# Cross-attention on Trainium2: a pair's transposes in front of the next pair's scores, with the exponentials and the normalising passes behind the values' copies

## The chip, the cores and the metric

The kernel runs on one core of a Trainium2 chip. A core has five engines that work side by side: TensorE (matmuls; its weight loads are listed apart, as PEld), VectorE (DVE), ScalarE (ACT), GpSimd (POOL) and SyncE (SP), which here issues the transfers. Each engine runs its own list of instructions in order and waits on semaphores for the others. TensorE writes its results into PSUM, eight banks of 128 x 512 fp32; the other data lies in SBUF, and the rest in the chip's memory. The metric is the device time of one execution in microseconds; lower is better.

## The reference, cut to what matters

There are 16 sequences of 64 tokens with 512 features, so 1024 tokens, and a context of the same shape. The computation is

```python
def attention(xn, ctx, bias, mask):              # xn: layer-normed x
    q, k, v = xn @ Wq, ctx @ Wk, ctx @ Wv        # 32 heads of 128
    s = einsum('bqhd,bkhd->bhqk', q, k) / sqrt(128) + bias
    s = where(mask, s, -inf)
    p = where(mask, softmax(s), 0)
    return einsum('bhqk,bkhd->bqhd', p, v).reshape(...) @ Wo   # 4096 -> 512

x = x + attention(layernorm(x), ctx, fside, mask)
# base product, plus experts of rank 16 that a router of 15 outputs weighs (its 8 largest)
x = x + ffn(layernorm(x))
```

Everything is fp32. Each sequence attends only to its own 64 context tokens, so scores and values are many small products (64 x 64 for each sequence and head), while the four projections of 512 to 4096 features and back are large ones.

## The kernel before, in words

**Products.** A large product is done in a split form: `split` (L69 to L71) writes the high part of an operand with a ScalarE cast (named `gh`, `wh`, `oh`, after what is split) and the remainder with a VectorE subtraction (`gl`, `wl`, `ol`), and `mm3` (L256) issues three 128 x 512 matmuls, high by high, low by high, high by low. In the profile these are the L259 matmuls. The projections to keys, values and queries use a scheme with seven products in place of eight on 2 x 2 blocks. One of the seven, for the queries of a pair of heads, is called here a query step: six matmuls of L259.

**Stages.** Up to about 328 us the keys and values of all 32 heads are computed and stored in the chip's memory (`kd`, `vd`). Then comes the attention loop of L563 to L604, over 16 pairs of heads, and from about 737 us the feed-forward part.

**A pair.** The weights of a pair's query product are loaded by `load_pair` and added and split on GpSimd, ScalarE and VectorE; `Queries` (L512) runs the seven steps, one for each call, copying partial results from PSUM with ScalarE (`u`, L530, and `q21`) or VectorE (`q`, L537). `scores` (L456) issues 16 small matmuls for a head into one bank from the pool `pss`, scales them and adds the bias with the mask (`bm`) on VectorE (L465), takes the row maxima (`nm`, L467), calls eight exponentials on ScalarE (L470; each also reads out its row sums into `sme`), and then normalises on VectorE: reciprocal (L473), times `valid` (L474), and the product p times rc (L475). `transpose_p` (L478) transposes a head's probabilities with four 128 x 128 transposes of TensorE into a bank of `pss`, and copies them out on ScalarE (`pt`). `pv_mm` (L487) multiplies them by the values with 32 small matmuls for a head into two banks of the pool `psp`, and splits the results (`oh`, `ol`). `proj_o` (L503) multiplies one tile of 128 tokens of a pair's results by that pair's part of Wo, two sets of three matmuls, and VectorE adds the bank to `acc` (L510). There are eight such tiles, `t` = 0 to 7. The profile counts two instructions for each small matmul of scores and values, so a pair has 64 and 128 of them.

**Order.** An iteration of the loop begins with the values of the previous pair (L566), whose results its `proj_o` calls use. Then it follows a string of letters: S is the scores of both heads of this pair, with their softmax, and after it the loads of the next pair's keys (`load_k`) and bias (`bias_of`); Q is one step of the next pair's queries; O is `proj_o` for the next tile; T is the transposes of one head. The third Q also loads this pair's rows of Wo (`load_o`, `wh`, `wl`), the seventh the weights of the pair after the next. The string is "QSQQQQQTQT" in the first pair, "QSQQOOQOQOOQOQOTTO" in all between, "SOOOOOOTOT" in the last. A Tile scheduler puts each engine's instructions in order by priority, which is program order except under `tc.high_priority(offset=...)`, where an instruction counts as that much earlier (SOON is 200). `tc.issue_after(x)` puts what is in its block behind instruction x on the engines. In the trace of a steady pair TensorE does, in this order: the values, a query step, the scores, query steps and Wo products mixed, the transposes of both heads, and a last Wo product.

**Banks and buffers.** `psp` has six banks, which rotate among queries, values and Wo products (`bank()`), `pss` has two. SBUF blocks are drawn from pools by tag (L40): ten `raw`, eight `sn` (scores p, their transposed form pt, and u), nine `o`, eighteen `g`, five `v`, and two `bm`.

Of the kernel before, what the change touches and what calls it, by code (L numbers as in the profile page):

```python
# [9 lines left out]
F32 = mybir.dt.float32  # L10
# [5 lines left out]
ALU = mybir.AluOpType  # L16
# [3 lines left out]
P = 128  # L20
# [4 lines left out]
S = 64  # L25
# [10 lines left out]
SOON = 200  # L36
# [11 lines left out]
def xattn_ffn_kernel(ctx: ExitStack, tc: tile.TileContext, x, ctxT, wq, wk, wv, wo, fside, mask,  # L48
                     base_wT, base_b, arT, router_b, lora_b, expert_map, out):
    nc = tc.nc  # L50
# [12 lines left out]
    def bank(k=None):  # L63
        return psp.tile([P, 512], F32, tag="ps", name="ps")

    def blk(tag, name, dt=F32, shape=(P, 512)):
        return pools[tag].tile(list(shape), dt, tag=tag, name=name)

    def split(hi, lo, src, lo_eng=None):  # L69
        nc.scalar.copy(hi, src)  # L70
        (lo_eng or nc.vector).tensor_tensor(lo, src, hi.bitcast(F32), ALU.subtract)  # L71

    valid = small.tile([P, NT], F32, name="valid")
    nhalf = small.tile([P, NT], F32, name="nhalf")
# [34 lines left out]
    with ExitStack() as actx:  # L109
# [6 lines left out]
        def small_bank(name):  # L116
            return pss.tile([P, 512], F32, tag="s", name=name)
# [138 lines left out]
        def mm3(o, stat, mov, first, last):  # L256
            (sh, sl), (mh, ml) = stat, mov
            for n, (a, b) in enumerate(((sh, mh), (sl, mh), (sh, ml))):
                nc.tensor.matmul(o, lhsT=a, rhs=b, start=first and n == 0, stop=last and n == 2,  # L259
                                 skip_group_check=True)  # L260
# [86 lines left out]
        with tc.manual_schedule(engines={nc.tensor.engine}):  # L347
# [3 lines left out]
            with tc.manual_schedule(engines={nc.tensor.engine, nc.vector.engine, nc.scalar.engine}):  # L351
                gs[0][1] = [blk("g", f"g{c}", F32R, (P, 2, 256)) for c in "hl"]
                tc_[1] = [tp.tile([P, 2, HALF], F32R, tag=f"t1{c}", name=f"t1{c}") for c in "hl"]
                hi, lo = tc_[1]
# [60 lines left out]
            acc = None  # L415
# [17 lines left out]
            def load_v(p):  # L433
                v = []
                for w in range(4):
                    v.append(blk("v", "v", F32, (P, 2, 256)))
                    nc.sync.dma_start(out=v[w], in_=vd[p // 2][:, p % 2, 2 * w:2 * w + 2, :])
                return v

            def load_o(p):  # L440
                w = []
                for i in range(2):
                    s = blk("raw", "so")
                    nc.sync.dma_start(out=s, in_=wo[p, i])
                    hl = [blk("g", f"w{c}", F32R) for c in "hl"]
                    split(hl[0], hl[1], s)
                    w.append(hl)
                return w
# [7 lines left out]
            def scores(qT, kT, bm):  # L456
                ps = small_bank("pss").rearrange("p (t s) -> p t s", t=NT)
                for t in range(NT):
                    for a in range(2):
                        n = 4 * (t // 2) + 2 * a + t % 2  # L460
                        c = slice((n % 8) * S, (n % 8 + 1) * S)
                        nc.tensor.matmul(ps[a * S:(a + 1) * S, t, :], lhsT=qT[n // 8][:, c],  # L462
                                         rhs=kT[n // 8][:, c], start=True, stop=True)
                p = blk("sn", "p", F32, (P, NT, S))
                nc.vector.scalar_tensor_tensor(p, ps, scale, bm, ALU.mult, ALU.add)  # L465
                nm = sm.tile([P, NT], F32, tag="nm", name="nm")
                nc.vector.tensor_reduce(nm, p, AX.X, ALU.max, negate=True)  # L467
                sme = sm.tile([P, NT], F32, tag="sme", name="sme")
                for t in range(NT):
                    nc.scalar.activation(p[:, t, :], p[:, t, :], AF.Exp, bias=nm[:, t:t + 1],  # L470
                                         accum_out=sme[:, t:t + 1])
                rc = sm.tile([P, NT], F32, tag="rc", name="rc")
                nc.vector.reciprocal(rc, sme)  # L473
                nc.vector.tensor_tensor(rc, rc, valid, ALU.mult)  # L474
                nc.vector.tensor_tensor(p, p, rc.unsqueeze(2).to_broadcast([P, NT, S]), ALU.mult)  # L475
                return p

            def transpose_p(p):  # L478
                ps = small_bank("pst")
                for g in range(4):  # L480
                    nc.tensor.transpose(ps[:, g * P:(g + 1) * P],  # L481
                                        p[:, 2 * g:2 * g + 2, :].rearrange("p t k -> p (t k)"), ident)
                pt = blk("sn", "pt", F32, (P, NT, S))
                nc.scalar.copy(pt, ps.rearrange("p (u q) -> p u q", q=S))
                return pt

            def pv_mm(i, pt, v, home="o"):  # L487
                ps = [bank() for _ in range(2)]
                for u in range(NT):
                    for b in range(2):  # L490
                        r = slice(b * S, (b + 1) * S)
                        for d in range(0, P, S):
                            c = slice(i * P + d, i * P + d + S)
                            nc.tensor.matmul(ps[b][d:d + S, u * S:(u + 1) * S], lhsT=v[u // 2][r, u % 2, c],  # L494
                                             rhs=pt[r, u, :], start=True, stop=True)
                res = []
                for b in range(2):
                    hl = [blk(home, f"o{c}", F32R) for c in "hl"]
                    split(hl[0], hl[1], ps[b])
                    res.append(hl)  # L500
                return res

            def proj_o(t, cts, w):  # L503
                ps = bank()
                b, g = divmod(t, 4)
                c = slice(g * P, (g + 1) * P)
                for i, ct in enumerate(cts):
                    mm3(ps, [a[:, c] for a in ct[b]], w[i], i == 0, i == 1)
                with tc.high_priority(offset=SOON):
                    nc.vector.tensor_tensor(acc[:, t, :], acc[:, t, :], ps, ALU.add)  # L510

            class Queries:  # L512

# [33 lines left out]
            qs = Queries(load_pair(0), ORDER_Q)  # L547
            tx = Tokens(xT, nc.gpsimd).all(ORDER_Q)
            acc = ax.tile([P, NT, D], F32, tag="ax", name="acc")
            for t in range(0, NT, 2):  # L550
                nc.sync.dma_start(out=acc[:, t:t + 2, :], in_=x[t:t + 2].rearrange("t p d -> p t d"))
            for n, i in enumerate(winograd(mm_weights(tc_, ops[len(stages) - 1]), 2, emit_k(NQ - 1), order=ORDER_Q)):
                if n == 3:
                    ks = [load_k(0), load_k(1)]
                    with tc.issue_after(stored[-1].ins):
                        bms = [bias_of(0), bias_of(1)]
# [2 lines left out]
            nxt = Queries(load_pair(1), ORDER_1)  # L559
            qs(1)  # L560
            NP = H // 2
            pts = v = w = prev = None
            for p in range(NP):  # L563
                last = p + 1 == NP
                if pts is not None:
                    prev = ([pv_mm(i, pts[i], v) for i in range(2)], w)  # L566
                v = load_v(p)
                after = None
                steps = "SOOOOOOTOT" if last else "QSQQOOQOQOOQOQOTTO" if p else "QSQQQQQTQT"
                pts, t, n = [], 0, 0  # L570
                for c in steps:
                    if c == "S":
                        ps = [scores(qs.head(i), ks[i], bms[i]) for i in range(2)]
                        if not last:
                            ks = [load_k(2 * p + 2 + i) for i in range(2)]
                            bms = [bias_of(2 * p + 2 + i) for i in range(2)]
                    elif c == "Q":
                        nxt(1)
                        n += 1
                        if n == 3:  # L580
                            w = load_o(p)
                        if n == 7 and p + 2 < NP:
                            after = Queries(load_pair(p + 2), ORDER)
                        if n == 7 and p + 2 == NP:
                            sar = [blk("raw", "sar", F32, (P, 2, NB)) for _ in range(2)]
                            sbw = [blk("raw", "sbw") for _ in range(KC)]
                            slb = blk("g", "slb")
                            nc.sync.dma_start(out=slb, in_=lora_b)
                            for i in range(2):
                                nc.gpsimd.memset(sar[i][:, :, NAR:NB], 0.0)  # L590
                                nc.sync.dma_start(out=sar[i][:, :, 0:NAR], in_=arT[:, 2 * i:2 * i + 2])
                            for kc in range(KC):
                                nc.sync.dma_start(out=sbw[kc], in_=base_wT[:, kc])
                    elif c == "T":
                        pts.append(transpose_p(ps[len(pts)]))
                    else:
                        proj_o(t, *prev)
                        t += 1
                        if last and t == 2:
                            w = load_o(p)  # L600
                qs, nxt = nxt, after
            now = ([pv_mm(i, pts[i], v, "g") for i in range(2)], w)
            proj_o(t, *prev)
            prev = now  # L604

# [122 lines left out]
    def out_norm(t):  # L728
        proj_o(t, *prev)
        ffn_norm(t)  # L730
# [27 lines left out]
    with tc.manual_schedule(engines=fixed | {nc.vector.engine}):  # L758
        for t in range(NT):
# [6 lines left out]
            n = 1 if t else 2  # L766
            po = bank()[:, 0:NF - NA]
            ffn_mm(po, *x2s[t], B, range(n))
            hh, hl = ffn_turn(hw)
# [52 lines left out]
```

## Time and profile before

| what | before |
|---|---|
| median of three runs | 778.54 us (777.83 to 778.75) |
| the profiled execution's own time | 779.41 us |
| its span, from first to last instruction | 777.6 us |
| TensorE busy | 770.8 us, 99%, 6314 matmuls |
| TensorE weight loads | 642.1 us, 83% |
| VectorE busy | 574.3 us, 74%, 1036 instructions |
| ScalarE busy | 413.6 us, 53%, 1165 instructions |
| GpSimd busy | 134.9 us, 17%, 143 instructions |
| granted TensorE clock | 0.997 of full speed |
| moved by DMA | 120.48 MB, 155 GB/s on average |

How to read it: a row of the timeline or of the groups has the start (or nothing), the busy time or mean, the engine, the line, the operation, what is written and what is read by the program's names, the tile's size and the count; a bracket gives idle time before it and what ended that. Matmuls are pipelined and their ends are modelled, so two of them overlap in the rows, and the distance from one start to the next tells what one costs. The weight load of the next matmul runs beside the matmul before. A row of the busy time by stretch gives the length and then, for TensorE, weight loads, VectorE, ScalarE and GpSimd, the busy time with the number of instructions, and last the granted clock, the share of time in which the DMA engines were busy, and GB/s. A row of the chain gives start, length, engine, tile, line and count.

### The profile page before, as it was taken

Reading aid. Unit: us, or ns where it says so; the run is one execution under the profiler, and the core shown is the slowest. Engines: PE = TensorE matmul, PEld = TensorE weight load, DVE = VectorE, ACT = ScalarE, POOL = GpSimd, SP = SyncE. Lnnn points to the kernel's source line nnn. Section 1 sums busy time; section 2 is a strip of 40 time slices with the busy share of each in tenths; the row PEclk is TensorE's granted clock in tenths of the full one; section 3 lists DMA queues with packets and bytes.
Section 4 is the critical chain, followed back from the end, with each engine's and each line's share of the span. In section 5 each row is a group of like instructions: output and inputs, shape, how many; then the busy total and the mean of one; then the engine's idle time right before and its main releaser. Section 6 shows DMA issues by size and latency. Waiting matters only on the chain.

```text
span 777.6 us, 16694 instructions
## 1 busy us (share of the span) xinstructions
PE 770.8 (99%) x6314; PEld 642.1 (83%) x6314; DVE 574.3 (74%) x1036; ACT 413.6 (53%) x1165; POOL 134.9 (17%) x143
## 2 busy tenths in 40 slices
PE   8999999999999999999999999999999999999998
PEld 6888887888888888887888888888888888888898
DVE  6986666665665756787877787778777877779875
ACT  5664454545454545575564556455645564556461
POOL 0000000000000522133330332033203320310330
PEclk9999999999999999999999999999999999999999
DMA  6695646464536345474554355435543544352011
GB/s 243 227 294 179 195 161 209 131 208 151 203 120 204 122 140 200 166 243 140 185 164 122 110 178 165 129 104 176 164 138 96 176 164 131 103 176 70 1 53 58
DMA packets 74705, 120.48 MB, mean 155 GB/s; under 512 B 7680, under 2 KB 24832, under 8 KB 74624
## 3 DMA queue, kind: packets, MB, share of 16 engines
q1 hardware_dynamic: 74480, 119.36, 46.7%
q8 instruction: 49, 0.80, 0.4%
q14 instruction: 32, 0.26, 0.1%
q10 hardware_dynamic: 144, 0.06, 0.0%
HBM read 83.74 MB, written 35.65 MB: 154 GB/s over the span
## 4 chain that ended last, share of the span: by engine, by line
PE 95%; DVE 3%; ACT 1%; DMA 1%; issue 0%; POOL 0%; SPq 0%; DVEq 0%; ACTq 0%; POOLq 0%
PE ps L259 74%; PE yz L259 5%; PE ps L668 5%; PE pss L462 4%; PE ps L494 4%; PE pst L481 2%; DVE gl L71 1%; ACT p L470 1%; DMA cT<-in_ctxT 1%; PE pst L104 0%; DVE bs L634 0%; DVE wl L71 0%; PE pt L104 0%; DVE ol L71 0%; DVE acc L510 0%
## 5 line engine op out<-in xcount | busy, mean ns | idle before, releaser
L70 ACT CAST gh<-s 128x512 fp32r<-128x512 f32 (+1 forms) x128 | 65.6, 515 | 121.1 <-PE ps L259 112.3
L470 ACT ACTIVATE p<-p,nm 128x64 f32<-128x64 f32 x256 | 85.5, 336 | 31.3 <-DVE nm L467 31.3
L259 PE MATMUL ps<-wh,oh 128*128 128x512 f32 x256 | 101.3, 396 | 0.0
L510 DVE TENSOR_TENSOR acc<-acc,ps 128x512 f32<-128x512 f32 x128 | 85.9, 681 | 20.2 <-PE ps L259 20.0
L259 PE MATMUL ps<-wh,ol 128*128 128x512 f32 x256 | 99.8, 390 | 0.0
L259 PE MATMUL ps<-wl,oh 128*128 128x512 f32 x256 | 99.8, 390 | 0.0
L71 DVE TENSOR_TENSOR gl<-s,gh 128x512 fp32r<-128x512 f32 (+1 forms) x128 | 71.5, 562 | 32.9 <-ACT gh L70 31.8
L161 POOL TENSOR_TENSOR s<-rq 128x256 f32<-128x256 f32 x32 | 27.6, 863 | 262.8 <-DMA rq<-in_wq 127.9
L71 DVE TENSOR_TENSOR gl<-raw,gh 128x512 fp32r<-128x512 f32 x48 | 34.5, 722 | 36.5 <-ACT gh L70 26.1
L259 PEld LDWEIGHTS ps<-wl,oh 128*128 128x128 f32 x256 | 48.0, 188 | 10.0
L259 PEld LDWEIGHTS ps<-wh,ol 128*128 128x128 f32 x256 | 48.1, 188 | 9.7 <-DVE ol L71 0.4
L259 PEld LDWEIGHTS ps<-wh,oh 128*128 128x128 f32 x256 | 48.1, 188 | 9.5
L70 ACT CAST gh<-raw 128x512 fp32r<-128x512 f32 x48 | 29.7, 622 | 48.3 <-PE yz L259 29.3
L453 POOL TENSOR_TENSOR bm<-bm,maskb 128x512 f32<-128x512 f32 x32 | 48.2, 1526 | 28.9 <-DVE rc L474 21.5
L470 ACT ACTIVATION_READ_ACCUMULATOR p<-p,nm 128x1 f32 x256 | 48.2, 188 | 0.0
L71 DVE TENSOR_TENSOR ol<-ps,oh 128x512 fp32r<-128x512 f32 x64 | 39.9, 682 | 10.3 <-ACT oh L70 10.3
L96 POOL TENSOR_TENSOR rs<-rs,nhalf 128x1 f32<-128x1 f32 x8 | 4.4, 551 | 246.1 <-DVE rs L95 246.1
L537 DVE TENSOR_TENSOR q<-u,ps 128x512 f32<-128x512 f32 x48 | 32.6, 680 | 9.2 <-PE ps L259 8.9
L70 ACT CAST oh<-ps 128x512 fp32r<-128x512 f32 x64 | 33.2, 591 | 11.6 <-PE ps L494 11.6
L71 DVE TENSOR_TENSOR gl<-rq,gh 128x256 fp32r<-128x256 f32 x48 | 26.9, 562 | 15.4 <-ACT gh L70 15.4
L462 PEld LDWEIGHTS pss<-kT,q 128*64 128x64 f32 x1024 | 31.3, 138 | 5.7 <-PE ps L259 5.2
L475 DVE TENSOR_TENSOR p<-p,rc 128x512 f32<-128x512 f32 x32 | 34.9, 1092 | 1.1
(260 smaller groups left out, 2015.8 us busy)
## 6 DMA issues: line engine op xcount, KB each, us to landing
kd<-c SPq DMA_DIRECT2D x64, 256.0 KB, 2.2
vd<-c SPq DMA_DIRECT2D x64, 256.0 KB, 2.6
kT<-kd SPq DMA_DIRECT2D x64, 256.0 KB, 5.0
v<-vd SPq DMA_DIRECT2D x64, 256.0 KB, 4.3
raw<-in_wk SPq DMA_DIRECT2D x32, 256.0 KB, 4.0
raw<-in_wv SPq DMA_DIRECT2D x32, 256.0 KB, 4.1
rq<-in_wq SPq DMA_DIRECT2D x32, 256.0 KB, 4.7
bm<-in_fside SPq DMA_DIRECT2D x32, 256.0 KB, 5.0
```

Of the source, the lines that this page charges most:

```text
L70: nc.scalar.copy(hi, src)
L71: (lo_eng or nc.vector).tensor_tensor(lo, src, hi.bitcast(F32), ALU.subtract)
L161: self.eng.tensor_tensor(r, a, b, op)
L259: nc.tensor.matmul(o, lhsT=a, rhs=b, start=first and n == 0, stop=last and n == 2, skip_group_check=True)
L453: nc.gpsimd.tensor_tensor(bm, bm, maskb, ALU.add)
L462: nc.tensor.matmul(ps[a * S:(a + 1) * S, t, :], lhsT=qT[n // 8][:, c], rhs=kT[n // 8][:, c], start=True, stop=True)
L470: nc.scalar.activation(p[:, t, :], p[:, t, :], AF.Exp, bias=nm[:, t:t + 1], accum_out=sme[:, t:t + 1])
L475: nc.vector.tensor_tensor(p, p, rc.unsqueeze(2).to_broadcast([P, NT, S]), ALU.mult)
L494: nc.tensor.matmul(ps[b][d:d + S, u * S:(u + 1) * S], lhsT=v[u // 2][r, u % 2, c], rhs=pt[r, u, :], start=True, stop=True)
L510: nc.vector.tensor_tensor(acc[:, t, :], acc[:, t, :], ps, ALU.add)
L537: nc.vector.tensor_tensor(self.blocks[key], s[u], b[bk], ALU.add)
L668: nc.tensor.matmul(o, lhsT=a, rhs=b, start=start, stop=stop, skip_group_check=True)
```

## The change

The transposes leave the end of an iteration and go to the front of the next one, directly before its scores. `scores` is cut in three: scaling and maxima stay, the exponentials become `exps`, the normalising pass becomes `normed`. The values become a letter of the string, P: they are computed after the scores and one query step, and the exponentials of both heads are issued behind the last of the values' casts (`evicted` holds the last cast and the last subtraction). Each head's normalising pass is issued behind the addition of a certain O to `acc`: the third O for the first head, the fifth for the second, and in the last pair the third and fourth. The transposes draw a bank of `psp` instead of `pss`; their copy and the values' copies get a higher priority. The loads of Wo rows are placed behind the values' copies. A lower-case o is an O of the pair before, left over to be issued after P; the pair before the last has five Os and the last pair takes over the rest. The number of matmuls, exponentials, copies and bytes stays as it was.

```diff
     def split(hi, lo, src, lo_eng=None):
-        nc.scalar.copy(hi, src)
-        (lo_eng or nc.vector).tensor_tensor(lo, src, hi.bitcast(F32), ALU.subtract)
+        first = nc.scalar.copy(hi, src)
+        return first, (lo_eng or nc.vector).tensor_tensor(lo, src, hi.bitcast(F32), ALU.subtract)
 
     valid = small.tile([P, NT], F32, name="valid")
     nhalf = small.tile([P, NT], F32, name="nhalf")
@@ -465,10 +465,16 @@
                 nc.vector.scalar_tensor_tensor(p, ps, scale, bm, ALU.mult, ALU.add)
                 nm = sm.tile([P, NT], F32, tag="nm", name="nm")
                 nc.vector.tensor_reduce(nm, p, AX.X, ALU.max, negate=True)
+                return p, nm
+
+            def exps(p, nm):
                 sme = sm.tile([P, NT], F32, tag="sme", name="sme")
                 for t in range(NT):
                     nc.scalar.activation(p[:, t, :], p[:, t, :], AF.Exp, bias=nm[:, t:t + 1],
                                          accum_out=sme[:, t:t + 1])
+                return p, sme
+
+            def normed(p, sme):
                 rc = sm.tile([P, NT], F32, tag="rc", name="rc")
                 nc.vector.reciprocal(rc, sme)
                 nc.vector.tensor_tensor(rc, rc, valid, ALU.mult)
@@ -476,13 +482,16 @@
                 return p
 
             def transpose_p(p):
-                ps = small_bank("pst")
+                ps = bank()
                 for g in range(4):
                     nc.tensor.transpose(ps[:, g * P:(g + 1) * P],
                                         p[:, 2 * g:2 * g + 2, :].rearrange("p t k -> p (t k)"), ident)
                 pt = blk("sn", "pt", F32, (P, NT, S))
-                nc.scalar.copy(pt, ps.rearrange("p (u q) -> p u q", q=S))
+                with tc.high_priority(offset=SOON):
+                    nc.scalar.copy(pt, ps.rearrange("p (u q) -> p u q", q=S))
                 return pt
+
+            evicted = []
 
             def pv_mm(i, pt, v, home="o"):
                 ps = [bank() for _ in range(2)]
@@ -496,7 +505,8 @@
                 res = []
                 for b in range(2):
                     hl = [blk(home, f"o{c}", F32R) for c in "hl"]
-                    split(hl[0], hl[1], ps[b])
+                    with tc.high_priority(offset=2 * SOON):
+                        evicted[:] = split(hl[0], hl[1], ps[b])
                     res.append(hl)
                 return res
 
@@ -507,7 +517,7 @@
                 for i, ct in enumerate(cts):
                     mm3(ps, [a[:, c] for a in ct[b]], w[i], i == 0, i == 1)
                 with tc.high_priority(offset=SOON):
-                    nc.vector.tensor_tensor(acc[:, t, :], acc[:, t, :], ps, ALU.add)
+                    return nc.vector.tensor_tensor(acc[:, t, :], acc[:, t, :], ps, ALU.add)
 
             class Queries:
 
@@ -559,25 +569,36 @@
             nxt = Queries(load_pair(1), ORDER_1)
             qs(1)
             NP = H // 2
-            pts = v = w = prev = None
+            ps, pts, t, w, prev = [], [], 0, None, None
+            v = load_v(0)
             for p in range(NP):
                 last = p + 1 == NP
-                if pts is not None:
-                    prev = ([pv_mm(i, pts[i], v) for i in range(2)], w)
-                v = load_v(p)
                 after = None
-                steps = "SOOOOOOTOT" if last else "QSQQOOQOQOOQOQOTTO" if p else "QSQQQQQTQT"
-                pts, t, n = [], 0, 0
+                steps = ("TTSOPooOOOOOOTOT" if last else "TTSQPQQQOOQOQOQO" if p + 2 == NP else
+                         "TTSQPQQQOOQOOQOOQOO" if p > 1 else "TSQPQQQOOQOOQOOQOO" if p else "QSQQQQQTQ")
+                n = 0
                 for c in steps:
-                    if c == "S":
-                        ps = [scores(qs.head(i), ks[i], bms[i]) for i in range(2)]
+                    if c == "P":
+                        old, told = prev, t
+                        prev, t = ([pv_mm(i, pts[i], v, "g" if last else "o") for i in range(2)], w), 0
+                        pts = []
+                        v = load_v(p)
+                        with tc.issue_after(evicted[0].ins):
+                            soft = [exps(*s) for s in ss]
+                    elif c == "S":
+                        ss = [scores(qs.head(i), ks[i], bms[i]) for i in range(2)]
+                        if not p:
+                            ps = [normed(*exps(*s)) for s in ss]
                         if not last:
                             ks = [load_k(2 * p + 2 + i) for i in range(2)]
                             bms = [bias_of(2 * p + 2 + i) for i in range(2)]
                     elif c == "Q":
                         nxt(1)
                         n += 1
-                        if n == 3:
+                        if n == 3 and p:
+                            with tc.issue_after(evicted[0].ins), tc.issue_after(evicted[1].ins):
+                                w = load_o(p)
+                        elif n == 3:
                             w = load_o(p)
                         if n == 7 and p + 2 < NP:
                             after = Queries(load_pair(p + 2), ORDER)
@@ -592,14 +613,21 @@
                             for kc in range(KC):
                                 nc.sync.dma_start(out=sbw[kc], in_=base_wT[:, kc])
                     elif c == "T":
-                        pts.append(transpose_p(ps[len(pts)]))
+                        pts.append(transpose_p(ps.pop(0)))
                     else:
-                        proj_o(t, *prev)
+                        if c == "o":
+                            proj_o(told, *old)
+                            told += 1
+                            continue
+                        added = proj_o(t, *prev)
                         t += 1
+                        if t in (3, 5 - last):
+                            with tc.issue_after(added.ins):
+                                ps.append(normed(*soft.pop(0)))
                         if last and t == 2:
                             w = load_o(p)
                 qs, nxt = nxt, after
-            now = ([pv_mm(i, pts[i], v, "g") for i in range(2)], w)
+            now = ([pv_mm(i, pts[i], v) for i in range(2)], w)
             proj_o(t, *prev)
             prev = now
```

## The prediction

> **What bounds the kernel now.** I read the busy table first, then the busy time by stretch, then the chain of work in order of time, then TensorE's and VectorE's own timelines.
>
> ```profile
> PE   770.8 (99%) x6314; PEld 642.1 (83%) x6314; DVE 574.3 (74%) x1036; ACT 413.6 (53%) x1165; POOL 134.9 (17%) x143
> ...
> PE 95%; DVE 3%; ACT 1%; DMA 1%; issue 0%; POOL 0%; SPq 0%; DVEq 0%; ACTq 0%; POOLq 0%
> ```
>
> ```profile
> 328.00:371.00 43.00, 42.32 (x538) 34.46 (x536) 33.66 (x59) 28.15 (x104) 13.78 (x12) 1.00 0.60 196
> 371.00:705.00 334.00, 334.00 (x3749) 277.92 (x3752) 264.43 (x440) 184.17 (x661) 76.96 (x78) 1.00 0.46 145
> ```
>
> The second fence has pairs 0 and 1, then pairs 2 to 14. In the second stretch TensorE is busy for all of 334.00 us; in the first it misses 0.68 us. A busy TensorE may still hide gaps, so I go by spacing of starts. The chain of one steady pair:
>
> ```profile
> 442.77 0.87 PE pst L481 x8
> 443.64 1.38 PE ps L259 x6
> 445.02 2.02 PE ps L494 x128
> 447.04 1.59 PE ps L259 x6
> 448.64 2.02 PE pss L462 x64
> 450.65 17.93 PE ps L259 x78
> 468.58 0.87 PE pst L481 x8
> ```
>
> The period is 25.81 us, TensorE alone, and it repeats to 0.01 us in almost every pair. The change keeps every matmul, so it can win only (1) waits and (2) gaps where one kind of matmul follows another. TensorE's timeline shows both:
>
> ```profile
> 361.24 0.39 PE L259 MATMUL ps<-wl,oh 128*128 128x512 f32 x1
> 362.31 0.50 PE L259 MATMUL ps<-t3h,gh 128*128 128x512 f32 x1 [0.68 <-DVE q L537]
> ...
> 520.05 1.03 PE L481 MATMUL pst<-ident,p 128*128 128x128 f32 x8
> 520.84 0.48 PE L259 MATMUL ps<-wh,oh 128*128 128x512 f32 x1
> 521.15 0.40 PE L259 MATMUL ps<-wh,ol 128*128 128x512 f32 x1
> 521.39 0.39 PE L259 MATMUL ps<-wl,oh 128*128 128x512 f32 x1
> ...
> 717.79 0.60 PE L481 MATMUL pst<-ident,p 128*128 128x128 f32 x4
> 718.31 0.40 PE L494 MATMUL ps<-pt,v 64*64 64x64 f32 x12
> ```
>
> Two 512-wide products normally start 0.227 us apart. From 361.24 to 362.31 is 1.07 us: a wait of 0.84 us in pair 1, the only one of that size between pair 0 and the last. The first transpose of a head starts 0.23 us after the product before it, so entering costs nothing. Eight transposes and two products take 521.39-520.05 = 1.34 us; less two products, 0.89; eight at 0.109 us are 0.87. So leaving the transposes costs 0.02 us.
>
> [...] (no later matmul filled the 0.84 us), so a late transpose stops all that stands behind it. [...] the normalising product took 0.69 us alone at 532.03 and 1.74 us at 535.59, while GpSimd ran from 535.49; the accumulation from PSUM at 533.82 kept 0.69.
>
> **The change, part by part.** Time 0 is the start of a pair's transposes; O is a Wo projection, Q a query step, each six products, 1.36 us.
>
> *Steady pairs, new order.* Transposes 0 to 0.87, scores 0.96 to 2.98, Q to 4.5, values 4.6 to 6.6, three Qs to 10.8, then the Os. The copies pt run from 0.63 (before: 520.68 against 520.05) to 1.7, and the values start at 4.6. The values' four oh copies began 1.19 us after the values before (523.58 against 522.39), so 5.8 to 7.9; the ol subtractions, 0.62 later, end at 8.9; the first O needs them at 10.8: 1.9 us to spare. Exponentials are now behind oh: 16 at 0.333 us spacing, with one u copy (0.5) among them, 7.9 to 13.8. Behind them on ScalarE: two wh casts to 14.8, then the third u copy, which cannot start before its Q ends at 14.9; it is done at 15.7, and the Q that overwrites its bank starts at 17.6. The wh serve the next pair. Normalising the first head follows the third O (16.3), the second the fifth O (20.3), ended by about 22.4; the next transposes are at 25.8 and 26.2. DMA: the score keys refill when the scores free them, or when the wl subtractions free a raw block, near 15.5, plus 5.0 us to land (DMA issues): 20.5 against 26.8. On SyncE the values' loads now stand behind bias and keys, whose waits are the scores at 3 and their bias pass at about 4; the values free their own blocks at 6.6, so nothing is held. GpSimd's sums and mask additions wait for rq, whose load follows the first head's scores at 2, and land near 7 to 13; what VectorE runs there reads PSUM. So I price the longer ScalarE queue at nothing, with 1.9 us of cover; if it were gone, each us past it is lost 13 times.
>
> *Gaps.* The 0.02 us of leaving the transposes goes, in 15 pairs: -0.3. Entering scores costs 0.10 (525.68 to 526.01, less 0.23). Transposes to scores stands nowhere in the trace. Nearest: transposes to values, 718.31-717.79 = 0.52, less 4 x 0.109: 0.085; I take 0.09, hence -0.01 a pair, -0.1 in all. Bounds: nothing to -1.5 us if transposes to scores were free.
>
> *Pair 1.* The wait of 0.84 us came from a late q on VectorE, behind wl and gl that were behind exponentials. Values now come first, the exponentials end near 353.4 instead of 355.6, and q22 near 356.5, before its step at 361: -0.84.
>
> *The pair before the last.* Its order string has only five Os, and the fifth is the last thing before the transposes. The second head's normalising pass is tied behind that O's accumulation, so the second head's transposes wait for VectorE. In VectorE's new order stand: accumulation, rc, a bl subtraction, rc times valid, a second bl, the product p. From the end E of the O: accumulation starts at E+0.20 (520.25 against 520.05), +0.60 to the next, rc 0.20, bl 0.60, rc 0.20, bl 0.60, p 0.69:
>
> ```profile
> 531.59 0.20 DVE L473 RECIPROCAL rc<-sme 128x8 f32<-128x8 f32 x1 [0.99 <-ACT p L470]
> 531.83 0.17 DVE L474 TENSOR_TENSOR rc<-rc,valid 128x8 f32<-128x8 f32 x1
> 532.03 0.69 DVE L475 TENSOR_TENSOR p<-p,rc 128x512 f32<-128x512 f32 x1
> ...
> 701.79 1.89 DVE L71 TENSOR_TENSOR bl<-sbw,bh 128x512 fp32r<-128x512 f32 x3
> ```
>
> Sum E+3.1, and a few hundredths to TensorE. The second head's transposes could have gone at E+0.44. TensorE waits 2.7 us; scores, values and all later work shift. Bounds: 1.5 without the two bl, 3.3 with a busy VectorE at E.
>
> *The last pair.* Values no longer touch scores: one more exit from scores (0.11) and entry into values (0.09): +0.2. Its exponentials run behind oh, and wl stands before the normalising pass; counted from the scores, the first head's p is ready about 0.4 us after its sixth O ends: +0.4 (0 to 0.8). Before, it had 1.1 us to spare.
>
> *After it* the feed-forward stage has the same order on every engine and starts later by the sum; it has no slack to absorb it, since its first products follow the last Os.
>
> Sum: -0.84 -0.3 -0.1 +2.7 +0.2 +0.4 = +2.06. The profiled span 777.6 becomes 779.7. That execution took 779.41, 1.8 around the span; the median of three, 778.54, stands 0.94 above the span. Forecast 780.6.
>
> **Rivals.** *Not slower, transposes to scores free:* place, each pair's seam; price -0.10 x 15 instead of -0.01 x 15: +0.7, 779.2. It decides from 0.033 us a pair more than I take. [...] Against: transposes to values is also such a seam and costs 0.085. *The late normalising pass is not felt* (the order on VectorE hides it): 777.9. Against: the pass can't precede the accumulation, and that can't precede the O; at least 1.5 us stays. *Grouping saves more than any row shows*, say 0.3 us a pair: 776.5. Nothing in the rows supports it; it is left as an unknown. *ScalarE becomes a bound in each pair:* if oh or u were late by 0.25 us past the cover, 13 times: 783.9. For it: 8.4 us of exponentials and read-outs now stand in the middle of the eviction copies. Against: the cover of 1.9 us worked out above.
>
> **Chances.** Forecast's case 0.54 (its own range 779.5 to 781.8; 0.44 of it above the bound), seam free or the late pass short 0.18, larger saving 0.14, a stall per pair 0.14. A measurement of this kernel can tell about 0.2%, 1.6 us, from no change, so slower 0.58, same 0.28, faster 0.14. The range reaches into the saving and into the stall: 777.0 to 783.6.
>
> **What would show it.** Right: steady period 25.79; no wait near 361; one TensorE gap of about 2.7 us between the two heads' transposes at the last pair's start, released by VectorE's normalising product; some 0.4 us before the last pair's first transposes. Wrong: a period below 25.7 (seam), a repeated wait for oh, ol or u (ScalarE), or no gap near the last pair.

## The result, and the profile after

The median of seven runs went from 778.75 us (777.83 to 779.65) to 780.89 us (779.12 to 782.4): ratio 1.0029, 95% interval 1.0019 to 1.0039, so 2.1 us slower. The forecast was 780.6. In a later comparison, under the experiments, the same two kernels stood at 1.0047 (1.0030 to 1.0063). The profiled execution took 780.89 us with a span of 779.1, against 779.41 and 777.6 before.

The busy table of the changed kernel and the shares of its chain:

```profile
PE 770.5 (99%) x6314; PEld 644.1 (83%) x6314; DVE 536.8 (69%) x1036; ACT 413.1 (53%) x1165; POOL 123.5 (16%) x143
...
PE 95%; DVE 2%; issue 1%; DMA 1%; SPq 0%; POOL 0%; DVEq 0%; ACT 0%; ACTq 0%; POOLq 0%
```

Every count is the same. VectorE is busy 37 us less, and the kernel is slower: what VectorE saved was off the path. The busy time by stretch, pairs 0 and 1 and then pairs 2 to 14 (columns as before: TensorE, weight loads, VectorE, ScalarE, GpSimd, then clock, DMA share, GB/s):

```profile
328.00:371.00 43.00, 43.00 (x598) 36.09 (x597) 31.80 (x61) 27.13 (x101) 12.72 (x13) 1.00 0.63 210
371.00:705.00 334.00, 331.62 (x3673) 277.27 (x3673) 230.02 (x440) 183.60 (x661) 66.89 (x77) 0.99 0.44 142
```

TensorE's idle time has moved. It was 0.68 us in the first stretch and nothing in the second; now the first has none, and the second has 2.38. A steady pair in the chain of work:

```profile
416.06 0.87 PE ps L487 x8
416.94 2.02 PE pss L462 x64
418.95 1.59 PE ps L259 x6
420.54 2.02 PE ps L503 x128
422.57 19.27 PE ps L259 x84
441.84 0.87 PE ps L487 x8
```

The period is 25.77 us; it was 25.81. The loss lies at the end of the pair before the last. TensorE's timeline there:

```profile
695.47 0.39 PE L259 MATMUL ps<-wl,oh 128*128 128x512 f32 x1
695.70 0.60 PE L487 MATMUL ps<-ident,p 128*128 128x128 f32 x4
698.60 0.66 PE L487 MATMUL ps<-ident,p 128*128 128x128 f32 x4 [2.29 <-DVE p L481]
699.18 3.22 PE L462 MATMUL pss<-kT,q 128*64 128x64 f32 x64
702.33 0.80 PE L259 MATMUL ps<-wh,oh 128*128 128x512 f32 x1
```

The second head's transposes start 2.90 us after the first's, where four take 0.44: a wait of 2.46 us, released by VectorE's p. VectorE's timeline shows why:

```profile
695.90 0.69 DVE L520 TENSOR_TENSOR acc<-acc,ps 128x512 f32<-128x512 f32 x1
696.51 0.20 DVE L479 RECIPROCAL rc<-sme 128x8 f32<-128x8 f32 x1
696.62 0.64 DVE L71 TENSOR_TENSOR bl<-sbw,bh 128x512 fp32r<-128x512 f32 x1
697.18 0.16 DVE L480 TENSOR_TENSOR rc<-rc,valid 128x8 f32<-128x8 f32 x1
697.25 0.69 DVE L71 TENSOR_TENSOR bl<-sbw,bh 128x512 fp32r<-128x512 f32 x1
697.86 0.69 DVE L481 TENSOR_TENSOR p<-p,rc 128x512 f32<-128x512 f32 x1
```

This is the predicted order. The fifth O ends at 695.70, its addition starts 0.20 later, and p is done at 698.55.

One more thing stands in TensorE's rows. Behind the wait, the 64 instructions of the scores take 3.22 us in place of some 2.08. The busy time by stretch gives the reason in its granted clock, 0.94, 0.50 and 0.70:

```profile
698.00:700.00 2.00, 1.40 (x28) 1.24 (x30) 2.00 (x4) 0.59 (x1) 0.00 (x0) 0.94 0.17 65
700.00:702.00 2.00, 2.00 (x44) 2.00 (x42) 1.50 (x3) 0.00 (x0) 0.00 (x0) 0.50 0.00 0
702.00:704.00 2.00, 2.00 (x14) 1.60 (x11) 1.60 (x3) 0.00 (x0) 0.00 (x0) 0.70 0.00 0
```

The lost clock is 2 x (0.06 + 0.50 + 0.30) = 1.72 us. No step of the prediction has this.

Where the time went, from the starts of the first scores, of the transposes after pair 1 and after pair 13, and of the last values. The changed kernel does one more O (1.36 us) before each of those transposes, which is taken off the second stretch and added to the last:

| stretch | before | after | difference |
|---|---|---|---|
| up to the first scores | 329.10 | 328.05 | -1.05 |
| to the transposes after pair 1 | 36.07 | 36.31 - 1.36 | -1.12 |
| to the transposes after pair 13 | 310.00 | 309.65 | -0.35 |
| to the last values | 43.14 | 46.03 + 1.36 | +4.25 |
| sum, last values' start | 718.31 | 720.04 | +1.73 |

The first row is no merit of the change, because TensorE's instructions up to there are the same. In the profile of before, the clock was 0.54 and 0.60 from 8 to 12 us, which costs 2 x (0.46 + 0.40) = 1.72 us of clock; in that of the changed kernel it was full there:

```profile
8.00:10.00 2.00, 2.00 (x6) 1.54 (x7) 1.76 (x3) 1.96 (x5) 0.00 (x0) 0.54 1.05 404
10.00:12.00 2.00, 2.00 (x7) 1.63 (x6) 2.00 (x4) 1.67 (x4) 0.00 (x0) 0.60 1.06 407
```

The last row is 2.46 of the wait, 1.55 of the low clock (from the second transposes to the next pass of transposes it took 717.66 - 698.60 = 19.06 us; a run below with the same work at full clock took 714.43 - 696.92 = 17.51), and 0.24 of the rest. Without the first row and the low clock, the change costs 1.23 us in these traces.

### The profile page after: what moved, and what is told of

Read it like the earlier page. It is cut to its first block, busy times and chain, and to the rows that moved or that the text cites. A ratio compares the mean times of both kernels' runs of the same rounds, so it can differ in the third digit from the quotient of the medians.

```text
span 779.1 us, 16614 instructions
## 1 busy us (share of the span) xinstructions
PE 770.5 (99%) x6314; PEld 644.1 (83%) x6314; DVE 536.8 (69%) x1036; ACT 413.1 (53%) x1165; POOL 123.5 (16%) x143
## 4 chain that ended last, share of the span: by engine, by line
PE 95%; DVE 2%; issue 1%; DMA 1%; SPq 0%; POOL 0%; DVEq 0%; ACT 0%; ACTq 0%; POOLq 0%
PE ps L259 74%; PE yz L259 5%; PE ps L696 5%; PE pss L462 4%; PE ps L503 4%; PE ps L487 2%; DMA cT<-in_ctxT 1%; PE pst L104 0%; DVE bs L662 0%; PE pt L104 0%; DVE acc L520 0%; DVE s L161 0%; POOL st L665 0%; DVE wl L71 0%; DVE t2l L71 0%
## 5 line engine op out<-in xcount | busy, mean ns | idle before, releaser
L520 DVE TENSOR_TENSOR acc<-acc,ps 128x512 f32<-128x512 f32 x128 | 87.5, 684 | 68.2 <-PE ps L259 67.7
L161 POOL TENSOR_TENSOR s<-rq 128x256 f32<-128x256 f32 x32 | 25.0, 780 | 260.0 <-DMA rq<-in_wq 223.5
L473 ACT ACTIVATION_READ_ACCUMULATOR p<-p,nm 128x1 f32 x256 | 52.3, 204 | 0.0
L540 ACT COPY u<-ps 128x512 f32<-128x512 f32 x48 | 28.1, 586 | 43.8 <-PE ps L259 41.6
L453 POOL TENSOR_TENSOR bm<-bm,maskb 128x512 f32<-128x512 f32 x32 | 41.8, 1323 | 33.0 <-DVE rc L480 22.0
L503 PEld LDWEIGHTS ps<-pt,v 64*64 64x64 f32 x2048 | 31.5, 135 | 5.8 <-issue 5.4
```

What stands on the lines that cost most here:

```text
L161: self.eng.tensor_tensor(r, a, b, op)
L453: nc.gpsimd.tensor_tensor(bm, bm, maskb, ALU.add)
L520: return nc.vector.tensor_tensor(acc[:, t, :], acc[:, t, :], ps, ALU.add)
L540: nc.scalar.copy(s[i], b["x"])
```

## Experiments

**The tie of the late pass.** In the pair before the last, the second head's normalising pass is put behind the fourth O.

```diff
-                        if t in (3, 5 - last):
+                        if t in (3, 5 - (p + 2 >= NP)):
```

> Theory (the late normalising pass): in the pair before the last the second head's pass now follows the fourth O, 2.72 us before the fifth ends, and needs 2.4 us less; both heads' transposes go in one block at the last pair's start, the wait of 2.46 us between them is gone, and the span falls from 779.1 to about 776.6 us, 0.3 to 1.0 us below the kernel before (ratio 0.9987 to 0.9996). Rival 1 (the transposes wait for a PSUM bank, not for VectorE): a wait of 2 us or more stays there, ratio 1.003. Rival 2 (the time is only passed on): the wait turns up at the last pair's scores or at its first transposes, and less than 1 us is won.

Measured: 776.83 us against 778.27, ratio 0.9981 (0.9975 to 0.9988), better than the forecast for it, and faster than both kernels. From 1.0029 to 0.9981, which are two comparisons, is 3.7 us, more than the wait of 2.46: the low clock went with it. TensorE's timeline has one block of eight transposes, and the scores follow at full clock:

```profile
696.03 0.39 PE L259 MATMUL ps<-wl,oh 128*128 128x512 f32 x1
696.26 1.03 PE L487 MATMUL ps<-ident,p 128*128 128x128 f32 x8
697.23 2.09 PE L462 MATMUL pss<-kT,q 128*64 128x64 f32 x64
```

No PSUM bank held the transposes, since the order on TensorE is the same. The wait did not turn up elsewhere. One comparison in a source line decides the sign of the whole change.

**The last pair as well.** On top of that, the last pair's rows of Wo are loaded three Os later.

```diff
-                        if last and t == 2:
+                        if last and t == 5:
```

> As the run with the fourth O, and the last pair's rows of Wo are loaded and split three Os later, so that VectorE's subtractions for them stand less in front of the last normalising passes. Theory: the 0.27 us before the last pair's first transposes go too: 0.3 us below the run with the fourth O, ratio to the kernel before 0.9983 to 0.9993. Rival: the passes wait for the exponentials on ScalarE, not for the subtractions: the 0.27 us stay.

Measured: 776.71 us against 778.27, ratio 0.9980 (0.9973 to 0.9987). In the changed kernel the last pair's first transposes started at 717.66, 0.50 us behind the product before them, where 0.23 is normal. Here:

```profile
713.25 0.39 PE L259 MATMUL ps<-wl,oh 128*128 128x512 f32 x1
713.48 0.60 PE L487 MATMUL ps<-ident,p 128*128 128x128 f32 x4
```

So the wait of 0.27 us is gone, and it came from the wl subtractions. The two medians are too close (0.12 us) to show it in time.

**The bl subtractions behind the pass.** The pass stays behind the fifth O, but the four splits of the feed-forward weights, the bl subtractions with their casts, are placed behind it (`normed_at` holds the last product p times rc).

```diff
+                            if p + 2 == NP:
+                                held[:] = normed_at
...
-        split(bh[:, kc, NB:NF], bl[:, kc, NB:NF], sbw[kc])
+        with tc.issue_after(held[0].ins):
+            split(bh[:, kc, NB:NF], bl[:, kc, NB:NF], sbw[kc])
```

> The four bl subtractions of the feed-forward weights are put behind the second head's normalising pass of the pair before the last; the pass stays behind the fifth O. Theory (the chain on VectorE, row by row): addition 0.61, rc 0.2, rc times valid 0.2, p 0.7 from 0.2 us after the O: the transposes wait 1.5 us in place of 2.46, and the span is about 778.1 us. Rival 1 (a PSUM bank): 2.46 us stay.

> The wait cut to 1.5 us of idle time by the bl subtractions put behind the pass. Theory (a lower clock follows only the longer idle time): clock 0.999 or more and 1.5 us above the run with the fourth O, near 778.2 us. Rival (any such wait brings it): clock 0.998, near 779.5 us.

TensorE's two transposes and VectorE's chain in the first of these runs:

```profile
694.94 0.60 PE L489 MATMUL ps<-ident,p 128*128 128x128 f32 x4
696.92 0.66 PE L489 MATMUL ps<-ident,p 128*128 128x128 f32 x4 [1.38 <-DVE p L483]
```

```profile
695.14 0.69 DVE L522 TENSOR_TENSOR acc<-acc,ps 128x512 f32<-128x512 f32 x1
695.75 0.20 DVE L481 RECIPROCAL rc<-sme 128x8 f32<-128x8 f32 x1
695.98 0.17 DVE L482 TENSOR_TENSOR rc<-rc,valid 128x8 f32<-128x8 f32 x1
696.18 0.69 DVE L483 TENSOR_TENSOR p<-p,rc 128x512 f32<-128x512 f32 x1
```

The wait is 1.98 - 0.44 = 1.54 us, as worked out, so the two bl in between cost 0.92. A single execution took 777.64 us, with a span of 775.9; the median of twenty was 778.99 against 778.19, ratio 1.0007 (1.0000 to 1.0015). In the first of the two profiles the clock did not fall behind the wait: the scores' 64 instructions took 2.08 us there, and the mean clock was 1.0. The mean clock of the timed runs was 0.999, as in the kernel before (8 of 20 had 0.998, against 7 of 27 with 0.998 or less). The median lies between the two forecasts, 778.2 and 779.5. In the same comparison the changed kernel stood at 782.59: a wait shorter by 0.92 us took 3.6 us away.

**The same tie in twelve pairs.** In the pairs 2 to 13 the second head's pass is put behind the eighth O.

```diff
-                        if t in (3, 5 - last):
+                        if t in (3, 5 - last if p + 2 >= NP or p < 2 else 8):
```

> In the pairs 2 to 13 the second head's normalising pass is put behind the eighth O in place of the fifth. Theory: the same wait in each of 12 pairs: addition 0.6, one gl of 0.4, rc 0.2, rc times valid 0.2, p 0.7, from 0.2 after the O, less the first head's 0.44 us: 1.9 us each, 22 us in all, span about 801 us; up to 2.9 us each (814 us) if p falls on GpSimd's work. Rival 2 (later work takes the time up again): less than 5 us in all.

> The kernel with 12 waits of 1.9 us and the one of 2.46 us, timed. In its one look no lower clock was seen. Theory 1 (the idle time of 2.3 us alone decides): mean clock 0.998 or less in most runs. Theory 2 (it decides only where TensorE ran without a break before): mean clock 0.999 to 1.0 in most runs. Median near 804 us either way.

Measured: 804.19 us in a single execution, span 802.4; the median of four was 803.86 against 778.52, ratio 1.0320 (1.0301 to 1.0339). One pair of the timed kernel's profile:

```profile
502.73 0.60 PE L487 MATMUL ps<-ident,p 128*128 128x128 f32 x4
505.05 0.66 PE L487 MATMUL ps<-ident,p 128*128 128x128 f32 x4 [1.72 <-DVE p L481]
```

The wait is 2.32 - 0.44 = 1.88 us in each of the twelve (expected 1.9), 22.6 in all: later work takes nothing of it up, because TensorE has no slack to do so. After the wait of 2.46 us near the end the clock was full in both profiles. Yet three of the four timed runs had a mean clock of 0.997 or 0.998, the profiled one with a fall near the start, where TensorE's products began 0.43 us apart from 19.55 to 22.54 us instead of 0.23. This does not tell the two theories on the clock apart.

**The transposes' bank.** The transposes take a bank of the pool of two again.

```diff
             def transpose_p(p):
-                ps = bank()
+                ps = small_bank("pst")
```

> The changed kernel with the transposes' bank from the pool of two again, which the scores use too. Theory: each head's scores then wait for the copy of that head's transposes, 0.6 us behind them; the second head's scores start near 1.7 us after the first transpose and not near 2.0, the first near 1.3 and not 0.96: 0.3 to 0.4 us a pair, 4 to 6 us in 15 pairs, span near 783 to 785 us. Rival: the copies are early enough, same span as the changed kernel within 1 us.

> The kernel with the transposes' bank in the pool of two, timed; a wait of 0.24 us idle in each pair and the one of 2.3 us near the end. Theory 1 (the idle time of 2.3 us alone decides): mean clock 0.998 or less in most runs, 785 us. Theory 2 (a break before prevents it): 0.999 to 1.0, 784 us.

Measured: 784.06 us in a single execution, span 782.2; the median of four was 784.55 against 778.52, ratio 1.0076 (1.0050 to 1.0102). In the single execution:

```profile
365.06 1.03 PE L487 MATMUL pst<-ident,p 128*128 128x128 f32 x8
366.34 1.85 PE L462 MATMUL pss<-kT,q 128*64 128x64 f32 x56 [0.24 <-ACT pt L491]
```

The scores start 1.28 us after the transposes, not 0.96, and the period is 26.08: 0.31 us in each pair, about 4 us. So it is the six-bank pool that lets the transposes stand directly in front of the scores without a wait for their copies. The second head's scores did not wait again. The profile of the timed kernel had the low clock behind the wait near the end (0.51 and 0.63 from 702 to 706), that of the single execution, with the same wait, had not; three of the four timed runs had a mean clock of 0.996 to 0.998. This settles only that the idle time does not decide alone.

**The exponentials not held.** They are issued without the tie to the values' casts.

```diff
-                        with tc.issue_after(evicted[0].ins):
-                            soft = [exps(*s) for s in ss]
+                        soft = [exps(*s) for s in ss]
```

> The changed kernel with the exponentials not held behind the values' copies: five of the sixteen now stand among the four oh casts on ScalarE. Theory (the cover of 1.9 us in each pair): the last oh ends 1.7 us later, no Wo product waits more than 0.2 us, and the period stays 25.77 to 25.9 us; so the queueing is worth next to nothing in time. Rival (ScalarE is near its bound): ol is late and TensorE waits 0.5 us or more in each pair, 7 us or more in all.

Measured: 779.52 us in a single execution, span 777.7, clock 0.999 and full behind the wait of 2.29 us. The period stays 25.77. In the pair whose transposes start at 518.81 the third ol, the last that the first O's need, ends at 529.29, and the O starts at 529.62. In the changed kernel all four were done at 528.2 for an O at 530.17. The cover shrank from 1.9 us to 0.3, and nothing waited but one product in the last pair (0.36 us). The queueing of the exponentials is worth next to nothing in time.

**The wait in pair 1.** In the kernel before, GpSimd's mask addition is left out for the two heads of pair 2 (their scores are then not masked).

```diff
-                nc.gpsimd.tensor_tensor(bm, bm, maskb, ALU.add)
+                if h not in (4, 5):
+                    nc.gpsimd.tensor_tensor(bm, bm, maskb, ALU.add)
```

> The kernel before, with GpSimd's mask addition left out for the two heads of pair 2 alone, whose scores are so not masked. It takes GpSimd's two additions away that ran beside VectorE from 357.9 to 361.0. Theory (q was late because wl, gl and p took 1.2, 1.5 and 1.2 us beside GpSimd instead of 0.7, 0.4 and 0.7): the wait of 0.84 us before 362.31 is gone, and q ends 1.5 to 2.5 us earlier against TensorE. Rival (what the prediction said alone, the exponentials in front of wl and gl): they still end at the same time, and 0.4 us or more of the wait stays.

Measured: 776.72 us in a single execution. VectorE in the kernel before, and then in this one:

```profile
358.38 1.51 DVE L71 TENSOR_TENSOR gl<-rq,gh 128x256 fp32r<-128x256 f32 x1
...
360.40 0.92 DVE L71 TENSOR_TENSOR gl<-rq,gh 128x256 fp32r<-128x256 f32 x1
361.25 0.41 DVE L71 TENSOR_TENSOR gl<-s,gh 128x256 fp32r<-128x256 f32 x1
361.58 0.67 DVE L537 TENSOR_TENSOR q<-u,ps 128x512 f32<-128x512 f32 x1
```

```profile
356.57 0.41 DVE L71 TENSOR_TENSOR gl<-rq,gh 128x256 fp32r<-128x256 f32 x1
...
357.50 0.41 DVE L71 TENSOR_TENSOR gl<-rq,gh 128x256 fp32r<-128x256 f32 x1
357.84 0.41 DVE L71 TENSOR_TENSOR gl<-s,gh 128x256 fp32r<-128x256 f32 x1
358.17 0.67 DVE L538 TENSOR_TENSOR q<-u,ps 128x512 f32<-128x512 f32 x1
```

The two gl beside GpSimd's additions took 1.51 and 0.92 us, alone 0.41. The product that had waited for q now starts at 359.75 without a gap, 0.9 us after q ends. From the first scores to the transposes after pair 1 it took 34.99 us in place of 36.07, 1.08 less: as much as the change itself gained there. The p and wl ahead of them stayed slow (1.17 and 1.23 us), because GpSimd's sums still ran beside them. So the collision was needed for the wait: full speed for the two gl was enough to end it. The exponentials stand further up in the same chain (in the kernel before they end at 355.65 and release the reciprocal at 355.68, from which VectorE works on without a break until q), but no run moved them alone, so their share is read from the rows and not shown by a run.

**A longer idle time.** In the pair before the last, three more VectorE operations (the maximum of p with itself) stand in front of the late product.

```diff
+                                    for _ in range(3):
+                                        nc.vector.tensor_tensor(pn, pn, pn, ALU.max)
                                 ps.append(normed(*soft.pop(0)))
```

> The changed kernel with three more VectorE operations (a maximum of p with itself) in front of the second head's product in the pair before the last: the idle time grows from 2.3 to about 4.1 us. Theory (the granted clock falls behind a long enough idle time): it falls in every run, mean clock 0.996 or less, and the time is 1.8 us above the changed kernel with its lower clock, or up to 1.6 more where that keeps its full clock. Rival (the lower clock has another cause): clock as in the kernel before in some of the runs.

Measured: 784.11 us against 778.52, ratio 1.0070 (1.0051 to 1.0089). TensorE idled for 4.16 us, and the clock fell behind it, to 0.83, 0.50 and 0.82 (1.70 us of lost clock). The four timed runs had mean clocks of 0.998, 0.995, 0.995 and 0.995; the expected 0.996 or less was missed by the profiled one. One such fall is worth 0.002 of the mean (1.70 of 781.9 us), so 0.995 stands for more than one. The changed kernel did not run beside this one, so the step of 1.8 us can only be read in the traces: the wait grew from 2.46 to 4.75 - 0.44 = 4.31.

**The changed kernel once more.**

> The changed kernel itself, once more, beside the kernel before. In its profile the granted clock fell to 0.5 and 0.7 in the 4 us behind the stall, which cost 1.5 us more. Theory (the lower clock follows the idle time of 2.3 us): this comes back in most runs; the mean granted clock of the runs stays at 0.998 or less, and the median is 3.5 to 4 us above the run with the fourth O, near 780.5 us. Rival (chance, or that chip): the clock is that of the kernel before, and the median is 2.5 to 2.9 us above it, near 779.5 us.

Measured: 782.59 us against 778.19, ratio 1.0047 (1.0030 to 1.0063). Its profile shows the same wait (2.30 us idle) and the same fall of the clock behind it:

```profile
700.00:702.00 2.00, 0.93 (x4) 0.63 (x4) 2.00 (x4) 0.43 (x1) 0.00 (x0) 0.80 0.34 131
702.00:704.00 2.00, 2.00 (x37) 1.97 (x38) 0.82 (x2) 0.58 (x1) 0.00 (x0) 0.50 0.00 0
704.00:706.00 2.00, 2.00 (x37) 1.81 (x34) 1.84 (x3) 0.00 (x0) 0.00 (x0) 0.84 0.00 0
```

The lost clock is again 1.72 us. All six runs had a mean clock of 0.995 to 0.998; the 27 of the kernel before beside it had 1.0 in most (7 of them 0.998 or less). In the first comparison six of seven runs of the changed kernel had 0.995 to 0.998. The seventh had 1.0 and took 779.12 us, only 0.4 us above that comparison's median for the kernel before. The expected median of 780.5 was missed by 2 us. The profiled run's mean clock of 0.996 stands for some 3.1 of its 781.6 us, an estimate (2.7 to 3.5 with the rounding of the mean), and the fall behind the wait for 1.72, so this wait is not the only thing that lowers the clock.

## Why the prediction was right

The mechanism and the place of the loss were forecast rightly. That the time came within 0.3 us is in part luck, because two misses partly cancel: the terms of the sum, +2.06, came out at +1.23, and 1.55 us of low clock, not in the sum, came on top.

- **The pair before the last, +2.7:** right in place, order and cause, 2.46 in size. From the O's end to p's end it took 2.85 us, not 3.1: rc to bl is 0.11 from start to start, and rc times valid to the second bl 0.07, where 0.20 each was taken from rows in which the next operation needs the result. The tie to the fourth O, the bl behind the pass and the twelve ties all gave what this working gives.
- **Pair 1, -0.84:** no wait is left near 361. The stretch gained 1.12, 0.28 more than the wait alone, and so did the run without the mask addition. The cause named, wl and gl behind exponentials, was not all of it: without GpSimd's mask addition beside gl there is no wait, and that collision the prediction had priced for p and not applied here.
- **Gaps, -0.4:** measured -0.04 us a pair, about -0.5. Transposes to scores are 0.96 us for eight, so 0.09 for the seam, as taken from transposes to values. The rival of a free seam falls.
- **The last pair, +0.4:** measured 0.27, and the wl subtractions are its cause, as written.
- **Values apart from scores, +0.2:** the price was right, but a gap of the kernel before, which the prediction did not see, went away beside it. From the last pair's transposes to its values the version without waits needs 715.84 - 695.87 = 19.97 us for two more Os than before (2.72), so 17.25, against 718.31 - 700.99 = 17.32 before. Its entries into scores and values and its exits from them cost 0.09, 0.10, 0.10 and 0.11 there. The kernel before paid 0.09 into the values, nothing from values to scores, and 0.10 out of the scores, so 0.21 less. But its second O behind the scores had a late ol: three starts there are 0.37 and 0.34 apart instead of 0.23 (the third product starts at 708.88), a gap of 0.25 us, seen again in the run without the mask addition (0.24).

```profile
703.33 2.09 PE L494 MATMUL ps<-pt,v 64*64 64x64 f32 x128
705.35 2.08 PE L462 MATMUL pss<-kT,q 128*64 128x64 f32 x64
...
708.17 0.40 PE L259 MATMUL ps<-wh,oh 128*128 128x512 f32 x1
708.54 0.50 PE L259 MATMUL ps<-wh,ol 128*128 128x512 f32 x1
```

- **ScalarE's longer queue, nothing:** right. The four ol end at 528.2 and the first O needs them at 530.17, 1.9 us to spare, the cover that was worked out.
- **The clock:** missing. The sum held TensorE's wait at its length, and did not ask what the array does afterwards.

## What to carry to other kernels

When TensorE has no slack, look at an edit's exceptional iterations first (first, last but one, last): thirteen regular pairs gave 0.04 us each, and one late tie took 2.46. A tie that is harmless behind the fifth of eight steps stalls where the fifth is the last, so count the time from the tie to its use in each variant of the order. Price an idle TensorE with the clock it may have afterwards (1.70 to 1.72 us lost here where it fell), and don't count busy time saved on an engine off the path (VectorE's 37 us here).

## What was not expected of the hardware

Behind some of TensorE's idle times its granted clock fell to 0.50, and each fall added up here costs 1.70 to 1.72 us of clock. The length of the idle time alone does not tell where that happens. Near the end, 2.3 us was enough in three of seven profiles that have such a wait (both of the changed kernel, and one of two with the transposes' bank in the pool of two), and 4.16 us in the one profile taken, while 1.38 us did not do it in the first profile with the bl behind the pass, nor did any of the 24 idle times of 1.72 us in the two profiles of the twelve ties.

No threshold follows from that, because near the start the clock also fell behind shorter idle times: 0.96 us before 7.18 in the kernel before (0.54 and 0.60 from 8 to 12 us), and 0.99 with 0.65 us behind it in the timed run of the twelve ties. In the first profile of the changed kernel 0.99 us before 7.54 left the full clock. What decides it was not shown by any run. Why nearly all timed runs of the changed kernel had a low clock, and not all of its variants with the same wait, stays open; the mean of a run does not say where in it the clock fell.

VectorE's 37 us have a cause in the rows of the groups. The product p times rc fell from 1092 to 688 ns on average, wl from 1055 to 702, and gl on 128 x 256 of rq from 562 to 429. In the rows they hardly run beside GpSimd any more: 25 of the 32 products p times rc did before, 1 of 32 does now. These three make 31.6 us of it, and none of that reached the end except in pair 1.

Several profiles have a gap of TensorE of 0.2 to 0.4 us inside the values or scores that nothing in the profile ends (0.36 in the changed kernel near 448 us, 0.24 in the kernel before near 554, 0.28 in the timed run with the bank in the pool of two near 632). From pair 2 to pair 13 each of the two kernels has it once. In the table above the third row has two such gaps, 0.36 us after and 0.24 before, so without them the change gained about 0.47 there, 0.04 in each of twelve pairs.
